# A two-layer cross-attention on one core: maxima transposed a slot later, even entries with their image tokens first, and one value product for two entries

## The chip, the cores and the metric

The kernel runs on one core of a Trainium2 chip. The time is device microseconds of one execution. The profile is of one execution of its own, whose time stands beside the others below.

## What is computed

Two cross-attention layers follow each other over 16 entries of 256 rows and 320 channels. Each entry has a context of 256 tokens of 512 channels. In layer 0 the first 77 tokens are text and the other 179 image tokens, with key and value weights of their own. In layer 1 252 are text and 4 image. The core of layer 0, from the reference (20 heads of 16 channels):

```python
q_h = _split_heads(q, B, HEADS, D)
k_h = _split_heads(k_text, B, HEADS, D)
probs = jax.nn.softmax(jnp.einsum('bhqd,bhkd->bhqk', q_h, k_h) * scale, axis=-1)
text_out = jnp.einsum('bhqk,bhkd->bhqd', probs, v_h)
scores = jnp.einsum('bhqd,bhkd->bhqk', q_h, ip_k_h) * scale
text_probs = jax.nn.softmax(jnp.einsum('bqc,bkc->bqk', q, k_text) * scale, axis=-1)
q_sem = jnp.einsum('bqk,bkc->bqc', text_probs, text)
sem = jnp.einsum('bqc,bnc->bqn', q_sem, ip) * scale
fused = scores + SEM_SCALE * sem[:, None, :, :]
ip_probs = jax.nn.softmax(fused, axis=-1) * spatial_mask[None, None, :, None]
ip_out = jnp.einsum('bhqk,bhkd->bhqd', ip_probs, ip_v_h)
out = (text_out + IP_SCALE * ip_out) @ Wout + bout + residual
```

So each head has two softmaxes over one row of scores, each with a maximum of its own, and the image scores get a term `sem` that is the same for all heads.

## The kernel before

Arithmetic is in f32 with most products split into a rounded high part and a remainder (`halves`, `split`, `evacuate`): a product of 128x320 over 512 channels is then a group of twelve matmuls (`prod`, L239).

**Slots.** A slot is one entry and one group of four heads. Layer 0 has slots 0 to 79 (five for an entry), layer 1 slots 80 to 159. `slot0(k)` writes one slot of layer 0 and does the work of three neighbours at once: the scores of slot k+2 in two halves (`score0`, L744) with the reduces that take their maxima over text and over image (DVE, L745 and L746), the transposed scores of slot k (`turned0`, L768), their `exp` (ACT, L771) and a product with the row factors (POOL, L774), and the attention of slot k−1 (`attend0`, L800, and `settle0`: DVE L811 to L817, POOL L818 and L820). The scores of `score0` have one tile of two banks, and the second half's scores use it after the first half's reduces.

**Maxima.** `maxima0(k)` transposes the reduced maxima on PE (L752), copies them on ACT (L754) and stores them with four transfers (L756, issued by ACT) into rows of the queries' stack Q. `turned0` of that slot then subtracts them in the same matmul. At the end of slot k the maxima of slot k+2 are handled, ahead of the background that is due by then. On ACT the second half's `exp` of slot k stays behind the four transfers of slot k+1 (`queued(exp, issues[k + 1])`).

**Background.** All other work of layer 0 is cut into steps with due times in slots (`task`, `fill`): of a pair of entries the keys (`keys0`), of an entry the queries (`queries0`, L609 and L612 on `hq`), token products `tokens0` of text with image tokens (tile M), the values (`values0_`: three groups of twelve matmuls for an entry, whose results ACT writes into the tile `vr`, L423), the semantic term (`semantic0`, L666, L685, L695), and the output projection (`close0`: L609 and L612 on `ho`, which ACT, then DVE split from the gathered attention at L282 to L284). A pair of entries takes ten slots, so the order of the background repeats every ten slots; "x2" below is slots 12, 22, 32 and so on. Context is loaded by pairs into tiles `cta` and `ctb` (`context`), split by ACT (L164) and POOL (L167). Keys go through a DRAM buffer (`kd`) into the stacks K (`ks`).

**What sets the order.** Up to slot 0 `begin()` is written out by hand, and every engine runs in the order written. In the slots, PE runs in the order written; the order of ACT, DVE, POOL and SP is chosen when the program is built, within what data and the edges of `anchor` and `queued` demand. An instruction marked `anchor` is one that later `queued` ones of its engine stay behind.

## Time and profile before

| | us |
|---|---|
| runs | 1503.99, 1501.08, 1503.84; median 1503.84 |
| profiled execution | 1502.55, span 1500.7, granted clock 0.990 |
| start-up (written out by hand) | 0 to about 66 of the span |
| slots 0 to 57 | about 66 to 515 |
| rest of layer 0 and the way into layer 1 | about 515 to 760 |

An engine in the profile runs its instructions in their order. A matmul waits for its operands at its place in the order of PE, so a wait that one shows is time in which PE does nothing. The name X is a tile of the matmul banks shared by the background work; S, T and P are the tiles of scores, of transposed scores, and of attention and probabilities. A tile's number in a name is left out by the profile, and kept in the rows of the order below.

### The profile page before, as it was taken

How to read it: one execution, taken by the hardware profiler on the slowest of the kernel's cores; microseconds unless marked ns; L12 is line 12 of the kernel's file. 1: busy time of each engine (PE TensorE's matmuls, PEld its weight loads, DVE VectorE, ACT ScalarE, POOL GpSimd, SP SyncE). 2: the span in 40 equal slices, each digit the busy share in tenths (PEclk: the TensorE clock that was granted, in tenths of full speed). 3: DMA queues.
4: the chain of work that ended last, by engine and by line, in shares of the span. 5: the costliest groups of instructions: out<-in, count | busy, mean ns of one | idle time of the engine just before them, and what ended most of it. 6: DMA issues, size and time to landing. Idle time of an engine off the chain costs nothing.

```text
span 1500.7 us, 36096 instructions
## 1 busy us (share of the span) xinstructions
PE 1422.2 (95%) x12740; PEld 1148.3 (77%) x12740; DVE 1179.7 (79%) x2593; ACT 889.5 (59%) x1975; POOL 1212.4 (81%) x1304
## 2 busy tenths in 40 slices
PE   8789999999999999789999999999999999999997
PEld 7678788888878877567777777777777777777765
DVE  5467777777778787878887788878877887788786
ACT  5356565656555655456665666566656665666563
POOL 4269797979787887898698779877987798779887
PEclk9799999999999999999999999999999999999999
DMA  7867777868676776774534434443444344433411
GB/s 234 202 200 211 199 221 196 226 190 223 185 207 193 219 217 167 199 214 145 165 99 130 124 116 118 131 128 112 121 131 128 110 122 127 130 109 99 121 30 44
DMA packets 230986, 234.32 MB, mean 156 GB/s; under 512 B 39127, under 2 KB 200678, under 8 KB 230790
## 3 DMA queue, kind: packets, MB, share of 16 engines
q1 hardware_dynamic: 228598, 230.71, 55.1%
q8 instruction: 102, 1.67, 0.5%
q10 hardware_dynamic: 2208, 1.30, 0.4%
q14 instruction: 78, 0.64, 0.1%
HBM read 118.04 MB, written 77.04 MB: 130 GB/s over the span
## 4 chain that ended last, share of the span: by engine, by line
PE 70%; DVE 13%; DMA 6%; POOL 5%; issue 3%; ACT 2%; SPq 1%; ACTq 0%; DVEq 0%; POOLq 0%
PE X L938 15%; PE X L239 14%; PE P L800 6%; PE X L609 5%; PE P L950 5%; PE P L960 4%; PE S L744 3%; PE T L890 3%; PE S L896 3%; DVE mn L746 3%; PE T L768 3%; PE X L612 2%; DVE nt L811 2%; PE X L578 2%; POOL P L774 1%
## 5 line engine op out<-in xcount | busy, mean ns | idle before, releaser
L774 POOL TENSOR_TENSOR P<-P,rs 128x512 f32<-128x512 f32 x320 | 413.7, 1314 | 89.8 <-ACT P L771 88.4
L929 POOL TENSOR_TENSOR wt<-P,ctb 128x512 f32<-128x512 f32 x320 | 410.7, 1307 | 74.0 <-ACT ctb L928 74.0
L938 PE MATMUL X<-ctb,gm 128*128 128x512 f32 x1120 | 305.4, 402 | 5.7 <-DVE wt L939 5.6
L771 ACT ACTIVATE P<-T 128x512 f32<-128x512 f32 x320 | 175.9, 595 | 151.1 <-PE T L768 120.6
L939 DVE TENSOR_TENSOR wt<-X,wt 128x512 f32<-128x512 f32 x320 | 216.5, 681 | 42.2 <-PE X L938 36.0
L938 PEld LDWEIGHTS X<-ctb,gm 128*128 128x128 f32 x1120 | 195.2, 188 | 39.0 <-DVE wt L939 8.6
L910 ACT ACTIVATE P<-T 128x512 f32<-128x512 f32 x320 | 173.2, 593 | 76.1 <-PE T L890 73.1
L928 ACT ACTIVATE ctb<-P 128x512 fp32r<-128x512 f32 x320 | 186.5, 627 | 38.9 <-PE X L938 33.5
L898 DVE TENSOR_REDUCE mn<-S 128x4 fp32r<-128x1008 f32 x160 | 191.5, 1197 | 0.0
L746 DVE TENSOR_REDUCE mn<-S 128x4 fp32r<-128x716 f32 x160 | 142.6, 891 | 0.0
L800 PE MATMUL P<-P,vr 128*32 128x256 f32 x1920 | 125.5, 392 | 7.2 <-DVE tmp L817 4.2
L744 PEld LDWEIGHTS S<-ks,qs 125*128 125x128 f32 x640 | 89.6, 194 | 39.9 <-issue 19.4
L744 PE MATMUL S<-ks,qs 125*128 125x256 f32 x640 | 114.4, 302 | 6.0 <-DMA ks<-M 3.7
L1027 POOL TENSOR_TENSOR r<-u,rs 128x40 f32<-128x40 f32 (+2 forms) x17 | 108.7, 6393 | 4.0 <-DVE u L1024 4.0
L745 DVE TENSOR_REDUCE mn<-S 128x4 fp32r<-128x308 f32 x160 | 74.9, 468 | 42.7 <-PE S L744 41.9
L768 PE MATMUL T<-qs,ks 127*128 127x256 f32 x640 | 105.5, 288 | 0.1
L800 PEld LDWEIGHTS P<-P,vr 128*32 128x32 f32 x1920 | 56.8, 112 | 48.2 <-issue 9.9
L768 PEld LDWEIGHTS T<-qs,ks 127*128 127x128 f32 x640 | 90.1, 194 | 0.9 <-issue 0.3
L950 PE MATMUL P<-P,v1t 128*32 128x256 f32 x1280 | 85.7, 385 | 0.0
L960 PE MATMUL P<-wt,zone 128*32 128x256 f32 x1280 | 84.6, 379 | 0.3 <-DVE wt L939 0.3
L811 DVE STREAM_TRANSPOSE nt<-P 128x512 f32<-128x512 f32 x80 | 57.0, 712 | 34.3 <-PE P L800 33.6
L239 PE MATMUL X<-wC,cta 128*128 128x324 f32 (+1 forms) x474 | 78.4, 312 | 0.0
(297 smaller groups left out, 2974.0 us busy)
## 6 DMA issues: line engine op xcount, KB each, us to landing
qd<-q SPq DMA_DIRECT2D x96, 256.0 KB
qs<-tph SPq DMA_DIRECT2D x64, 320.0 KB
rawc<-in_cT_dram SPq DMA_DIRECT2D x60, 256.0 KB
qs<-qd SPq DMA_DIRECT2D x80, 192.0 KB
ks<-kd SPq DMA_DIRECT2D x80, 192.0 KB
ks<-kd SPq DMA_DIRECT2D x160, 96.0 KB
qs<-qd SPq DMA_DIRECT2D x160, 96.0 KB
kd<-kst SPq DMA_DIRECT2D x57, 256.0 KB
```

What stands on the lines that cost most here:

```text
L239: last = mm(out, lhs(a, k), rhs(b, k), start=i == 0, stop=i == len(terms) - 1)
L744: mm(sp[:, h], Q[: XROW + T0, h, t * 128 : (t + 1) * 128], K[: XROW + T0, h], start=True, stop=True)
L746: anchor(nc.vector.tensor_reduce(mn[:, t, :, 1], sp[:, :, T0:], axis=AX.X, op=ALU.max))
L768: mm(st[p][:, j], K[:KS0, 2 * p + j, t * 128 : (t + 1) * 128], Q[:KS0, 2 * p + j], start=True, stop=True)
L771: exp = anchor(nc.scalar.activation(pt, st[p], AF.Exp, scale=SCALE))
L774: anchor(nc.gpsimd.tensor_mul(pt, pt, rs[:, t : t + 1].to_broadcast([128, 2, S])))
L800: mm(pv[32 * s : 32 * s + 32, o : o + S], v[:, vt, h : h + 32], P[k, s // 2][:, t, s % 2], start=vt < 2, stop=vt != 1,)
L898: anchor(nc.vector.tensor_reduce(maxes[k + 2][:, t], sp[:, :, :T1], axis=AX.X, op=ALU.max))
L928: nc.scalar.activation(R[k, u][:, t], P[k, u][:, t], AF.Copy, scale=0.5)
L929: anchor(nc.gpsimd.tensor_sub(W[k, u][:, t], P[k, u][:, t], f(R[k, u][:, t])))
L938: mm(yp, gm[:, gb], R[k, u][:, kt], start=i == 0, stop=i == len(blocks[n]) - 1)
L939: nc.vector.tensor_mul(W[k, u][:, n], yp, W[k, u][:, n])
```

## The change

Five parts, all of them in layer 0:

1. **Maxima.** For slots 1 to 57 (`SOON`) the maxima of slot k+1 are handled as the first thing of slot k, after the background of the slot before, in place of the maxima of slot k+2 ahead of the background of slot k. From slot 57 on they are handled as before.
2. **Image first.** Even entries have their image tokens ahead of their text in the key stack (a view 77 columns further on, `turned_ks`, of a stack that is 77 columns wider), in the reduces, in the product with M, and in the order of the three value tiles in `attend0`.
3. **One product for two mixed tiles.** An entry's 256 tokens make a tile that has the text, a mixed one and one of image tokens alone for the value products. With the even entry turned around, the mixed tiles of both entries are the same 128 columns of the context tile, and one product serves both: `values_mixed` is one group of twelve matmuls, evicted twice with different masks (`emask`, `tmask`). A pair of entries needs five groups and not six. `mark` writes the masks' columns for an entry, where `marks` did it once.
4. **Context and keys by piece.** Context tiles are padded, with text at one place and images at another, so a loaded context tile is split in two pieces, by ACT and POOL, with edges between them. Image keys are evicted per entry in two pieces on ACT and DVE (128x179), and POOL copies the text keys for an entry at a time. The token product has 180 columns in place of 192, the text keys' product 154 in place of 156.
5. **Start-up.** `fields()` stores the ends of the wider stacks with four more transfers; the constants of the padded tiles are set by more than 20 small memsets on POOL. `tokens0` sets no columns to zero in the slots any more.

The core of the diff:

```diff
     def slot0(k):
+        if 0 < k <= SOON:
+            yield lambda: maxima(k + 1)
         yield lambda: ahead(k + 2, 0)
         yield lambda: turned0(k, 0)
         yield 0.2
...
         yield 0.6
-        yield lambda: maxima(k + 2)
+        if k >= SOON:
+            yield lambda: maxima(k + 2)
         yield 1.0
...
-        for t, (w,), lo, sc in ((0, wv0, 0, tmask[:, 0:1]), (1, wvi0, 0, tmask[:, 1:2]), (2, wvi0, 128, 1.0)):
-            vp = bank()[:, :320]
-            prod(vp, lambda s, k: ct(s, k)[:, i, lo : lo + 128], lambda s, k: w(s, k), 4)
+    def value_rows(ct, at, w, *to):
+
+        vp = bank()[:, :320]
+        prod(vp, lambda s, k: side(ct[k], s, at, 128), lambda s, k: w(s, k), 4)
+        for V, t, sc in to:
             nc.scalar.activation(
...
+    def values_mixed(c):
+        to = [(vr[(b + 2) % 3], 1, masks(b)[1]) for b in (2 * c, 2 * c + 1)]
+        value_rows(ct0[c], CI + 128, wvi0[0], *to)
+        yield
...
+    def evacuate(hi, lo, out, m, pieces=None):
+
+        cut = [lambda t, b=b: t[:, b] for b in pieces] if pieces else [lambda t: t]
+        if m == 2:
+            hi, lo = hi[:64], lo[:64]
+            both = buf("both", list(hi.shape), bufs=2)
+        for of in cut:
+            nc.scalar.copy(of(hi), of(out[:64] if m == 2 else out))
+        if m == 2:
+            nc.scalar.copy(both, out[64:])
+            out = out[:64]
+        for of in cut:
+            nc.vector.tensor_sub(of(out if m == 2 else lo), of(out), f(of(hi)))
+        if m == 2:
+            nc.vector.tensor_add(lo, out, both)
...
+        if loaded == "pieces":
+            order = lambda inst: anchor(queued(inst))
...
+                hi, lo, src = ahead.pop(0)
+                if isinstance(hi, list):
+                    for piece in zip(hi, lo, by_side(src)):
+                        halves(*piece, eng, "pieces")
...
-        task(("v0", 2 * c), shifted(n, -7, -5.4, -5), lambda b=2 * c: values0_(b), *k)
-        task(("v0", 2 * c + 1), shifted(n, -4, -3.8, -3.4), lambda b=2 * c + 1: values0_(b), *k)
+        task(("v0", 2 * c), shifted(n, -7, -5.4), lambda b=2 * c: values0_(b), *k)
+        task(("vm", c), shifted(n, -4.2), lambda c=c: values_mixed(c), *k)
+        task(("v0", 2 * c + 1), shifted(n, -3.8, -3.4), lambda b=2 * c + 1: values0_(b), ("vm", c))
```

**PE at the end of slot 29.** L752 (after: L845) is the transposes of the maxima, L685 (L776) a transpose of the semantic term, L609 (L700) a query projection; each row ends with the shape of one result and the count. Before, and then of the change:

```order
L768 MATMUL T<-qs_96,ks_100 128x256 x4
L752 MATMUL X<-ident_r,mn_567 8x128 x2
L685 MATMUL X<-ident,sp_376 77x128
L685 MATMUL X<-ident,sp_377 77x128
L609 MATMUL X<-hq_230,wE_86 128x256 x8
```
```order
L861 MATMUL T<-qs_96,ks_100 128x256 x4
L776 MATMUL X<-ident,sp_413 77x128
L776 MATMUL X<-ident,sp_414 77x128
L700 MATMUL X<-hq_270,wE_86 128x256 x8
L845 MATMUL X<-ident_r,mn_615 8x128 x2
```

The transposes of the maxima have moved behind the ten matmuls of the background. They now stand directly ahead of the scores of the next slot.

**PE at the end of slot 34.** L239 (L251) with the weights `wD` is the value products. Before, and then of the change:

```order
L768 MATMUL T<-qs_97,ks_101 128x256 x4
L239 MATMUL X<-wD,cta_81 128x320 x3
L239 MATMUL X<-wD,cta_82 128x320 x3
L239 MATMUL X<-wD,ctb_83 128x320 x3
L239 MATMUL X<-wD,ctb_84 128x320 x3
L752 MATMUL X<-ident_r,mn_566 8x128 x2
L239 MATMUL X<-wD,cta_81 128x320 x3
L239 MATMUL X<-wD,cta_82 128x320 x3
L239 MATMUL X<-wD,ctb_83 128x320 x3
L239 MATMUL X<-wD,ctb_84 128x320 x3
```
```order
L861 MATMUL T<-qs_97,ks_101 128x256 x4
L251 MATMUL X<-wD,cta_81 128x320 x3
L251 MATMUL X<-wD,cta_82 128x320 x3
L251 MATMUL X<-wD,ctb_83 128x320 x3
L251 MATMUL X<-wD,ctb_84 128x320 x3
L845 MATMUL X<-ident_r,mn_614 8x128 x2
```

One of two value groups is gone from this place, and the transposes stand at the end.

**DVE from slot 31 into slot 32.** L811 (after: L907) is the transpose of an attention result, L745 and L746 (L838 and L839) the reduces, L814, L815 and L817 (L910, L911 and L913) the rest of `settle0`, L830 (L926) gathers attention for the output projection, L283 and L284 (L326 and L327) split its operand `ho`, L260 and L261 (L276 and L278) evict the third part of keys and queries. The last two rows of before are the reduces of slot 32's first scores:

```order
L745 TENSOR_REDUCE mn_567<-S 128x4
L746 TENSOR_REDUCE mn_567<-S 128x4
L814 RECIPROCAL P<-nt_136 128x16
L283 TENSOR_TENSOR ho_161<-hT_1308,ho_161 128x512
L284 SCALAR_TENSOR_TENSOR ho_161<-ho_161,tmask,hT_1308 128x256
L815 TENSOR_TENSOR P<-P,mk 128x8
L260 TENSOR_TENSOR X<-X,kst_160 64x2x179
L817 TENSOR_TENSOR tmp_807<-nt_136,P 128x256
L745 TENSOR_REDUCE mn_566<-S 128x4
L746 TENSOR_REDUCE mn_566<-S 128x4
```

In the change the reduces of slot 32's first scores are the seventh and eighth row (tile `mn_614`), and the first row is the last reduce of slot 31:

```order
L839 TENSOR_REDUCE mn_615<-S 128x4
L910 RECIPROCAL P<-nt_137 128x16
L911 TENSOR_TENSOR P<-P,mk 128x8
L913 TENSOR_TENSOR tmp_850<-nt_137,P 128x256
L926 STREAM_TRANSPOSE hT_1337<-hsn 128x256
L276 TENSOR_TENSOR X<-X,kst_194 64x179
L838 TENSOR_REDUCE mn_614<-S 128x4
L839 TENSOR_REDUCE mn_614<-S 128x4
L276 TENSOR_TENSOR X<-X,kst_194 64x179
L276 TENSOR_TENSOR X<-X,q_146 64x256
L326 TENSOR_TENSOR ho_195<-hT_1337,ho_195 128x512
L327 SCALAR_TENSOR_TENSOR ho_195<-ho_195,tmask,hT_1337 128x256
```

`ho` has moved from ahead of slot 32's first reduces to behind them and behind two subtractions. PE's projection that reads it stands in slot 32 behind the first transposed scores, as before.

**DVE from slot 37 into slot 38.** L846 (after: L942) adds bias and residual of the output projection; the eviction of the queries' third part, L260 and L261 (L276 and L278), is read by the semantic product L666 (L757) of slot 38. Before, and then of the change:

```order
L817 TENSOR_TENSOR tmp_807<-nt_136,P 128x256
L260 TENSOR_TENSOR X<-X,q_145 64x256
L846 SCALAR_TENSOR_TENSOR xc_116<-X,bo,xc_116 128x256
L261 TENSOR_TENSOR q_145<-X,both_281 64x256
L745 TENSOR_REDUCE mn_566<-S 128x4
L746 TENSOR_REDUCE mn_566<-S 128x4
L846 SCALAR_TENSOR_TENSOR xc_116<-X,bo,xc_116 64x256
```
```order
L913 TENSOR_TENSOR tmp_850<-nt_137,P 128x256
L942 SCALAR_TENSOR_TENSOR xc_117<-X,bo,xc_117 128x256
L838 TENSOR_REDUCE mn_614<-S 128x4
L839 TENSOR_REDUCE mn_614<-S 128x4
L276 TENSOR_TENSOR X<-X,q_146 64x256
L942 SCALAR_TENSOR_TENSOR xc_117<-X,bo,xc_117 64x256
L278 TENSOR_TENSOR q_146<-X,both_319 64x256
```

L261 stood ahead of the reduces of slot 38's first scores; as L278 it stands behind them, behind L276 and the third part of L942.

More of the change, by code (lines that the diff above doesn't have):

```diff
@@ L394, in keys_first @@
         out = lambda lo, hi: bank()[:, : 2 * (hi - lo)].rearrange("p (b t) -> p b t", b=2)
-        kp = [out(0, T0 + 1) for m in range(3)]
+        kp = [out(0, T0) for m in range(3)]
         for k in range(4):
@@ L399, in keys_first @@
                 for i, (a, c) in enumerate(terms):
-                    mm(kp[m], wk0(a, k, m), ct(c, k)[:, :, : T0 + 1], start=k + i == 0, stop=k == 3 and i == len(terms) - 1)
+                    mm(kp[m], wk0(a, k, m), texts_of(ct[k], c), start=k + i == 0, stop=k == 3 and i == len(terms) - 1)
             yield
@@ L803, in values0 @@
                 P[k, s // 2][:, t, s % 2],
[L804 to L805 removed]
+                start=bool(start),
+                stop=bool(stop),
             )
```

185 lines of the change are left out of this document (119 added, 66 removed).

## Prediction

> **What bounds the kernel now.** I read the page's head and its shares of the chain first, then the busy time by stage, then PE's waits in the stage that the change touches.
>
> ```profile
> PE 1422.2 (95%) x12740; PEld 1148.3 (77%) x12740; DVE 1179.7 (79%) x2593; ACT 889.5 (59%) x1975; POOL 1212.4 (81%) x1304
> ...
> PE 70%; DVE 13%; DMA 6%; POOL 5%; issue 3%; ACT 2%; SPq 1%; ACTq 0%; DVEq 0%; POOLq 0%
> ```
>
> PE is busy 95% of the span and carries 70% of the chain, DVE 13%. By stage (columns: stretch, length, then busy time of PE, PEld, DVE, ACT and POOL, the granted clock, the DMA share, GB/s):
>
> ```profile
> 0.00:66.00 66.00, 48.38 (x286) 45.11 (x287) 34.17 (x97) 32.38 (x83) 23.46 (x45) 0.90 0.83 233
> 66.00:515.00 449.00, 428.50 (x4023) 366.54 (x4023) 338.98 (x773) 259.02 (x599) 371.36 (x361) 1.00 0.73 203
> ```
>
> The second row holds slots 0 to 57 of the first layer, where the changed order lies. PE idles 20.5 us of 449 there, POOL is busy 83%, DVE 75%. The second layer's order is left as it is. What PE waits for in slots 0 to 57 (us in total, times, longest):
>
> ```profile
> PE X L752 <- DVE mn L746: 12.3, 22, 0.8
> ...
> PE S L744 <- DVE mn L746: 0.2, 1, 0.2
> ```
>
> Over half of the idle time is the transposes of the maxima waiting for the reduces of the scores ahead of them. So there are two ways to gain: fewer matmuls, and that wait. There is one large way to lose: another engine's result that PE now meets too early.
>
> **The maxima, moved.** One such wait, at the end of slot 29, PE first and DVE after it:
>
> ```profile
> 295.06 0.22 PE L752 MATMUL X<-ident_r,mn 128*8 128x128 f32 x1
> 296.12 0.23 PE L752 MATMUL X<-ident_r,mn 128*8 128x128 f32 x1 [0.84 <-DVE mn L746]
> 296.18 0.39 PE L685 MATMUL X<-ident,sp 128*77 128x128 f32 x2
> 296.33 1.18 PE L609 MATMUL X<-hq,wE 128*128 128x256 f32 x8
> 297.35 0.64 PE L744 MATMUL S<-ks,qs 125*128 125x256 f32 x4
> ```
> ```profile
> 295.17 0.90 DVE L746 TENSOR_REDUCE mn<-S 128x4 fp32r<-128x716 f32 x1
> ```
>
> The second transpose waits 0.84 us for a reduce that ends at 296.07. In the new order the ten matmuls of L685 and L609 stand ahead of both transposes: 297.35 − 296.18 = 1.17 us of cover. The reduce is then done, and the wait goes. The other slots of the ten-slot cycle get their background group in front in the same way. I take the whole row: **−12.3 us**. The bounds are 0 (the wait turns up elsewhere) and −12.3. The four transfers that follow (L756) leave later, and `exp` of the slot's second half is queued behind them on ACT; the TURN that needs them comes most of a slot later, and a slot lasts 7.8 us (from slot 32 to 38 in the rows below, 359.23 − 312.29 for six). That is why I cost this delay at nothing. If the cover were thinner than I think, each late landing would stop TURN.
>
> **Fewer matmuls.** The value groups in slot 34, and the token group behind them:
>
> ```profile
> 331.80 1.04 PE L239 MATMUL X<-wD,cta 128*128 128x320 f32 x6
> ...
> 333.57 0.29 PE L752 MATMUL X<-ident_r,mn 128*8 128x128 f32 x2
> 333.69 1.10 PE L239 MATMUL X<-wD,cta 128*128 128x320 f32 x6
> ...
> 335.50 0.64 PE L744 MATMUL S<-ks,qs 125*128 125x256 f32 x4
> ...
> 336.46 0.70 PE L239 MATMUL X<-cta 128*77 128x192 f32 x6
> ...
> 337.62 1.07 PE L800 MATMUL P<-P,vr 128*32 128x256 f32 x16
> ```
>
> A group of twelve 320-column matmuls takes 333.57 − 331.80 = 1.77 us, or 335.50 − 333.69 = 1.81. Eight groups go, one for each pair of entries; the first lies in the start-up stretch, where PE waits for transfers anyway. Seven times 1.81 rounded up for the issue between groups is **−12.9 us**. The evictions stay as many, since each entry still gets its own. The token group takes 337.62 − 336.46 = 1.16 us for 192 columns; at 180 it is 12/192 of that, 0.07 us, for 14 groups; **−0.9 us** with the text keys' 154 columns in place of 156.
>
> The gains sum to 12.3 + 12.9 + 0.9 = **26.1 us**.
>
> **What now waits for DVE: the output projection.** The order of DVE has changed most at slots 12, 22, 32, 42 and 52. Slot 32 in the trace of before:
>
> ```profile
> 312.29 0.63 PE L744 MATMUL S<-ks,qs 125*128 125x256 f32 x4
> ...
> 313.25 1.43 PE L609 MATMUL X<-ho,wF 128*128 128x256 f32 x8
> ...
> 315.10 1.27 PE L800 MATMUL P<-P,vr 128*32 128x256 f32 x18 [0.43 <-DVE tmp L817]
> ```
> ```profile
> 311.29 1.39 DVE L283 TENSOR_TENSOR ho<-hT,ho 128x512 fp32r<-128x512 f32 x1
> 312.60 1.52 DVE L284 SCALAR_TENSOR_TENSOR ho<-ho,tmask,hT 128x256 fp32r<-128x256 f32 x1
> ```
>
> DVE starts `ho` at 311.29, a microsecond before slot 32 begins, so the projection L609 runs almost unhindered. In the new order `ho` stands behind the reduces of slot 32's own scores and two subtractions of 64 rows. How soon the reduces end after their scores is seen where DVE idled before them, in slot 37:
>
> ```profile
> 352.00 0.64 PE L744 MATMUL S<-ks,qs 125*128 125x256 f32 x4
> ```
> ```profile
> 353.08 0.90 DVE L746 TENSOR_REDUCE mn<-S 128x4 fp32r<-128x716 f32 x1
> ```
>
> That is 353.98 − 352.00 = 1.98 us after the scores start. So in slot 32: 312.29 + 1.98 = 314.27. The two subtractions and `ho` cost:
>
> ```profile
> L260 DVE TENSOR_TENSOR X<-X,q 64x256 f32<-64x256 f32 x17 | 7.1, 420 | 7.3 <-ACT both L259 7.3
> ...
> L260 DVE TENSOR_TENSOR X<-X,kst 64x154 f32<-64x154 f32 x7 | 2.2, 318 | 5.5 <-ACT both L259 5.5
> ...
> L283 DVE TENSOR_TENSOR ho<-hT,ho 128x512 fp32r<-128x512 f32 x16 | 21.4, 1336 | 7.2 <-ACT ho L282 7.2
> ...
> L284 DVE SCALAR_TENSOR_TENSOR ho<-ho,tmask,hT 128x256 fp32r<-128x256 f32 x16 | 15.9, 995 | 0.0
> ```
>
> With about 0.08 us of each overlapping the next, these are 0.32 + 0.34 + 1.26 + 0.95 = 2.9 us, so `ho` is complete near 317.2 (317.7 with the 1.52 us that L284 took in this slot). The projection's last matmuls take another half microsecond, and the attention L800 starts at 317.7 to 318.2 in place of 315.10: **2.6 to 3.1 us, taken as 2.9, in five slots: +14.5 us.** The bounds are 0 a slot (if the scheduled order is not what holds PE) and 3.1.
>
> **A second, smaller wait of that kind** lies at slots 8, 18, 28, 38 and 48. Slot 38 before:
>
> ```profile
> 359.23 0.64 PE L744 MATMUL S<-ks,qs 125*128 125x256 f32 x4
> ...
> 360.77 0.79 PE L666 MATMUL X<-kb,q 128*128 128x156 f32 x6
> 361.50 1.50 PE L800 MATMUL P<-P,vr 128*32 128x256 f32 x24
> ```
> ```profile
> 360.04 0.41 DVE L261 TENSOR_TENSOR q<-X,both 64x256 fp32r<-64x256 f32 x1
> ```
>
> The sixth matmul of L666, near 361.37, reads what L261 has written by 360.45. In the new order L261 comes behind the reduces of slot 38's scores (359.23 + 1.98 = 361.21), a subtraction of 0.42, L846 of 0.46 and its own 0.41, less 0.08 each: it ends near 362.35. That is 1.0 us late, five times: **+5.2 us** (bounds 0 and 6). The even entries' `ho` also moves to the end of slot x6, where the second half's scores of slot x7 can wait for the reduces behind it, 0 to 0.4 us each: **+1 us**.
>
> **Start-up.** Four more transfers are issued on SP's queue within a stretch that runs without a gap and lies on the chain:
>
> ```profile
> 18.00 3.67 SPq L84 DMA_DIRECT2D ks<-mt  x4
> ```
>
> Four like them are 3.67 us. SP is in the chain in pieces between landings, so I take about half, **+2.0 us** (bounds 0 and 3.7). The additional small memsets and context pieces run on POOL and ACT, which are busy 23 and 32 of those 66 us.
>
> **The rest costs nothing where it is hidden.** Keys in two pieces instead of one give ACT and DVE a second short operation each, on engines with at least a quarter idle; what that does to their order is counted above. POOL gets more: the context subtraction in two pieces, two small copies an entry, twice the key copies, less one memset.
>
> ```profile
> POOL P L774 <- ACT P L771: 60.1, 60, 4.7
> ```
> ```profile
> L384 POOL CAST kb<-kst 128x308 fp32r<-128x308 f32 x14 | 6.2, 441 | 0.0
> ...
> L820 POOL COPY hsn<-hsn 128x128 f32<-128x128 f32 x16 | 4.8, 302 | 0.8
> ```
>
> From the last two rows a column costs (441 − 302)/(308 − 128) = 0.77 ns, so the fixed part of an operation is some 0.2 us. Four pieces, four copies and three key copies, less two memsets, are nine of these, 1.8 us in a cycle of ten slots. POOL has 17% of 78 us free, 13 us, and most of that is waiting for `exp` (60.1 of the 77.6 us that it idles in this stretch, first row). I count nothing; the bounds are 0 and the price under the rivals.
>
> **The sum.** Losses: 14.5 + 5.2 + 1.0 + 2.0 = 22.7 us. Net −26.1 + 22.7 = **−3.4 us** against the profiled execution's 1502.55 us (span 1500.7): 1499.2. The median of the runs is 1503.84, 1.3 above that execution; on it the forecast is **1500.5 us**.
>
> **A page against the trace.** Alone in the start-up, a DVE subtraction of 128x512 with two SBUF inputs takes 692 ns, while the same shape in L283 takes 1336 with POOL at work:
>
> ```profile
> L1263 DVE TENSOR_TENSOR cta<-rawc,cta 128x512 fp32r<-128x512 f32 x2 | 1.4, 692 | 3.4 <-ACT cta L1256 3.4
> ```
>
> The Trainium skill, page "SBUF — State Buffer", section "SBUF: two separate sides", says that DVE and GpSimd share one pair of ports as an exclusive lock, and that the loser waits until the whole instruction is done. The two rows agree with it. By that rule POOL, which runs out of work while PE stands still in slots 12 to 52, would leave the port to `ho`, which would then cost 0.65 us less: 5 × 0.65 = 3.2 us less loss, 1497.3. I do not take it, since POOL has `exp` of the same slot to multiply at that moment. The same skill, page "Perfetto Trace Analysis", section "Optimizing Scalar/DVE Operations", says that breaking up instructions may let work complete sooner where an engine isn't saturated but causes bubbles; that speaks for the pieces and against my costing their order as a loss.
>
> **The rivals.**
>
> *The gains arrive whole.* DVE and PE shift against each other, `ho` comes early enough, and only the start-up is lost: 1503.84 − 26.1 + 2.0 = **1479.7 us**. For it: DVE is only 75% busy in this stretch. Against it: an engine runs its list in order, and the list has `ho` behind reduces that can't start before slot 32's scores. Chance 0.15; half of the losses would give 1491.
>
> *POOL becomes the bound (the slower side).* In slots 25 to 29 it works almost without a gap, and its lead over PE is small:
>
> ```profile
> 285.75 5.21 POOL L774 TENSOR_TENSOR P<-P,rs 128x512 f32<-128x512 f32 x4
> ```
> ```profile
> 292.57 1.50 PE L800 MATMUL P<-P,vr 128*32 128x256 f32 x24
> ```
>
> Slot 28's products end at 290.96 and its attention starts at 292.57: 1.6 us ahead. In such a stretch PE would gain about 2.2 of a cycle's 26.1/7 = 3.7 us, and POOL be charged 1.8; from 1.6 us on, each further microsecond stops PE. That gives back 4.0 − 1.6 = 2.4 us a cycle, and in four cycles (the first starts with POOL ahead) 9.6 us: **1510.1 us**. Against it: PE's new stalls at x2 and x8 give POOL time. Chance 0.17.
>
> *The change doesn't remove the wait.* The score tile has one buffer, so the next scores need the same reduces that the maxima waited for; the wait moves to L744: +12.3, **1512.8 us**. Against it: those scores wait 0.2 us in all today, behind 1.2 to 1.8 us of other matmuls. Chance 0.08.
>
> *The maxima land late.* Transfers issued up to 1.8 us later hold TURN or ACT's queue, 0.1 us a slot: 57 × 0.1 = 5.7, **1506.2 us**. Chance 0.10.
>
> **How the numbers follow.** My forecast has 0.50. Its own terms reach from 1490 (the `ho` stall at half) to 1506 (a start-up at 3.7, later waits at their bounds). The range goes from 1485 to 1511: of the cases outside it, the whole gain and the wait that only moves, about 0.2 is left out. A difference of 0.2%, 3 us, is what a measurement can tell from none. Faster by more (below 1500.8): half of the forecast, 0.27, the first rival 0.15, and a few of the rest, 0.46. Within: 0.20 of the forecast and 0.07 of late maxima, 0.27. Slower (above 1506.8): 0.17 + 0.08 and the tail, 0.27.
>
> **What would show it.** In the trace of the changed kernel, the wait of the maxima's transposes for the reduces should be gone up to slot 57 and stay beyond it. The projection reading `ho` should wait for DVE some 2.9 us in slots 12, 22, 32, 42 and 52; the product with the text keys (L666 in before) about 1 us in slots x8. PE should have 96 matmuls fewer. The start should be 2 us longer up to the first attention. If `ho` does not hold PE, or POOL's idle time falls under 5% in slots x5 to x9, the prediction is wrong by that term.

## The result, and the profile after

| | before | changed |
|---|---|---|
| median (lowest to highest), us | 1502.88 (1501.08 to 1505.82) | 1514.45 (1508.53 to 1516.88) |
| profiled execution: time, span, granted clock | 1502.55, 1500.7, 0.990 | 1508.53, 1506.8, 0.982 |

The ratio is 1.0060, with an interval of 1.0045 to 1.0074: the change costs about 9 us by the ratio (the medians lie 11.6 us apart). The forecast was 1500.5, and the range ended at 1511. The profiled execution of the changed kernel is the fastest of its six, so a second trace of the same program, 1516.7 us long, stands beside it below ("the change again").

From the page of the changed kernel: the first row has the engines' busy time, the second their shares of the chain.

```profile
PE 1420.0 (94%) x12644; PEld 1144.5 (76%) x12644; DVE 1173.7 (78%) x2625; ACT 888.6 (59%) x2031; POOL 1223.0 (81%) x1391
...
PE 70%; DMA 11%; DVE 8%; POOL 3%; issue 3%; ACT 2%; SPq 2%; ACTq 1%; DVEq 0%; POOLq 0%
```

PE has 96 matmuls fewer, as forecast, yet is busy only 2.2 us less. The busy time by stage, in the columns of before, says why:

```profile
0.00:66.00 66.00, 48.23 (x270) 45.36 (x271) 34.12 (x107) 32.99 (x94) 24.40 (x73) 0.84 0.80 227
66.00:515.00 449.00, 423.88 (x3952) 362.06 (x3952) 334.57 (x791) 257.28 (x638) 378.08 (x411) 0.98 0.76 203
```

In slots 0 to 57 the idle time grew from 20.5 to 25.1 us, and the clock fell from 1.00 to 0.98: part of the work that is left runs slower. The waits of PE in that stage:

```profile
PE X L700 <- ACT ho L325: 6.3, 5, 1.3
PE X L251 <- DVE sp L760: 2.7, 1, 2.7
PE X L757 <- ACT mt L847: 2.5, 2, 1.3
PE X L700 <- DVE ho L326: 2.3, 5, 0.5
PE X L757 <- DVE q L278: 2.2, 3, 0.8
PE S L836 <- DMA qs<-mt: 1.9, 2, 1.1
...
PE T L861 <- DMA qs<-mt: 1.1, 3, 0.6
```

The wait of the maxima's transposes, 12.3 us in 22 waits of at most 0.8, is gone in this trace. In its place stand fewer and longer ones: the output projection (L700), the text keys' product (L757), one wait of 2.7 us (L251) that no step had, and 3.0 us for the transfers of the maxima, for which the kernel before does not wait here at all.

To see where the time went I cut each trace into windows of half a microsecond and added up three things: time in which PE did nothing, PE's busy time multiplied by (1 − granted clock), and the rest, which is the matmuls at full clock.

| profiled execution, us | span | PE idle | lost to half clock | matmuls at full clock |
|---|---|---|---|---|
| before | 1500.7 | 77.7 | 13.4 | 1409.7 |
| changed | 1506.8 | 86.2 | 24.0 | 1396.8 |
| the change again | 1516.7 | 91.6 | 27.1 | 1397.9 |
| forecast difference | | +10.4 | 0 | −13.8 |
| measured differences | | +8.5, +13.9 | **+10.6, +13.7** | −12.9, −11.8 |

Two columns came out near the forecast, the idle time of the second trace 3.5 us above it. The column of half clock was not in the sum at all.

By place: at the attention of slot 57 the changed kernel's first trace is 1.0 us behind before (0.9 of it from the start-up), where the forecast's terms, less the one product group that comes later, have it 1.6 us ahead; the second trace is 8.7 us behind. The rest, 5.1 and 7.3 us, comes later, and 4.3 and 2.7 us of that in layer 1, whose order the change leaves as it is. Why layer 1 took longer is not shown.

**One long wait, row by row.** In slot 9 of the changed kernel, PE first, then DVE, then POOL:

```profile
141.00 2.15 PE L251 MATMUL X<-cta,wB 128*128 128x360 f32 x6 [2.72 <-DVE sp L760]
```
```profile
136.88 3.92 DVE L327 SCALAR_TENSOR_TENSOR hq<-hq,tmask,xq 128x256 fp32r<-128x256 f32 x1
140.73 0.22 DVE L760 TENSOR_TENSOR sp<-sp,X 128x77 f32<-128x77 f32 x1
```
```profile
133.63 5.01 POOL L867 TENSOR_TENSOR P<-P,rs 128x512 f32<-128x512 f32 x4
138.60 1.25 POOL L326 TENSOR_TENSOR hq<-xq,hq 128x512 fp32r<-128x512 f32 x1
139.82 0.45 POOL L914 TENSOR_TENSOR hsn<-tmp 128x128 f32<-128x128 f32 x1
140.22 0.31 POOL L464 CAST kb<-kst 128x154 fp32r<-128x154 f32 x1
```

DVE's L327 is a short operation: on the same shape it takes 0.47 us in slot 32 below. Here it lasts 3.92 us and ends when POOL's gapless row of seven instructions ends (140.22 + 0.31 = 140.53). The small subtraction that PE needs stands behind it. What follows on PE (columns as in the stages above, clock third from the end):

```profile
140.00:141.00 1.00, 0.00 (x0) 0.00 (x0) 1.00 (x4) 0.00 (x0) 0.53 (x2) 1.00 0.93 146
141.00:142.00 1.00, 1.00 (x3) 1.00 (x4) 1.00 (x4) 0.94 (x3) 0.34 (x2) 0.53 1.00 197
142.00:143.00 1.00, 1.00 (x5) 1.00 (x5) 0.73 (x3) 0.60 (x2) 1.00 (x1) 0.50 0.71 203
143.00:144.00 1.00, 1.00 (x5) 1.00 (x4) 0.16 (x1) 0.24 (x2) 1.00 (x2) 0.50 0.01 2
145.00:146.00 1.00, 1.00 (x24) 0.49 (x16) 0.59 (x2) 0.71 (x3) 0.00 (x0) 1.00 0.00 0
```

PE works again from 141.0, but at half clock until about 144.5. The wait is 2.72 us; with the half clock, and a wait of 0.84 us for L278 ahead of it, slots 8 and 9 came out 5.3 us longer.

**The forecast stall, row by row.** Slot 32, where the projection was to wait 2.9 us. PE, then DVE:

```profile
316.19 0.64 PE L861 MATMUL T<-qs,ks 127*128 127x256 f32 x4
318.08 0.39 PE L700 MATMUL X<-ho,wF 128*128 128x256 f32 x1 [1.26 <-ACT ho L325]
318.92 1.08 PE L700 MATMUL X<-ho,wF 128*128 128x256 f32 x7 [0.45 <-DVE ho L326]
```
```profile
316.80 0.88 DVE L839 TENSOR_REDUCE mn<-S 128x4 fp32r<-128x716 f32 x1
317.61 0.33 DVE L276 TENSOR_TENSOR X<-X,kst 64x179 f32<-64x179 f32 x1
318.20 0.67 DVE L326 TENSOR_TENSOR ho<-hT,ho 128x512 fp32r<-128x512 f32 x1
318.80 0.47 DVE L327 SCALAR_TENSOR_TENSOR ho<-ho,tmask,hT 128x256 fp32r<-128x256 f32 x1
```

The order was as forecast: `ho` behind the reduces of the same slot. The wait is 1.26 + 0.45 us, not 2.9. The first matmul waits for ACT's part of `ho` (0.83 us, behind the copy of the maxima), which the forecast had left out, and DVE then does its two parts in 0.67 and 0.47 us where I took 1.26 and 0.95. POOL was waiting for `exp` from 317.3 to 318.6 and then began its own product. The Trainium skill's rule that I set aside (page "SBUF — State Buffer", section "SBUF: two separate sides") was the right one in this slot: 0.67 us for an operation that began while POOL stood idle, against 1336 ns on average before. POOL's own product, which started at 318.60 while DVE held on, took 1.82 us in place of 1.28.

### The profile page after: what moved, and what is told of

It reads as the page before. It is cut to its first block, busy times and chain, and to the rows that moved or that the text cites. A ratio compares the mean times of both kernels' runs of the same rounds, so it can differ in the third digit from the quotient of the medians.

```text
span 1506.8 us, 36169 instructions
## 1 busy us (share of the span) xinstructions
PE 1420.0 (94%) x12644; PEld 1144.5 (76%) x12644; DVE 1173.7 (78%) x2625; ACT 888.6 (59%) x2031; POOL 1223.0 (81%) x1391
## 4 chain that ended last, share of the span: by engine, by line
PE 70%; DMA 11%; DVE 8%; POOL 3%; issue 3%; ACT 2%; SPq 2%; ACTq 1%; DVEq 0%; POOLq 0%
PE X L1034 15%; PE X L251 12%; PE P L896 6%; PE X L700 6%; PE P L1046 5%; PE P L1056 4%; PE S L836 4%; PE S L992 3%; PE T L986 3%; PE T L861 3%; DMA qs<-mt 3%; PE X L261 2%; PE X L669 2%; DMA ks<-kd 2%; PE X L703 1%
## 5 line engine op out<-in xcount | busy, mean ns | idle before, releaser
L839 DVE TENSOR_REDUCE mn<-S 128x4 fp32r<-128x716 f32 x160 | 142.4, 890 | 0.0
L836 PE MATMUL S<-ks,qs 125*128 125x256 f32 x640 | 119.4, 310 | 9.0 <-DMA ks<-kd 2.4
L836 PEld LDWEIGHTS S<-ks,qs 125*128 125x128 f32 x640 | 89.9, 197 | 45.2 <-issue 25.1
L838 DVE TENSOR_REDUCE mn<-S 128x4 fp32r<-128x308 f32 x160 | 75.0, 469 | 34.8 <-PE S L836 34.3
L907 DVE STREAM_TRANSPOSE nt<-P 128x512 f32<-128x512 f32 x80 | 57.1, 713 | 54.2 <-PE P L896 53.7
L700 PE MATMUL X<-ho,wF 128*128 128x256 f32 x512 | 75.0, 287 | 10.7 <-ACT ho L325 7.2
```

The source lines that it names most:

```text
L836: mm(sp[:, h], Q[: XROW + T0, h, t * 128 : (t + 1) * 128], K[: XROW + T0, h], start=True, stop=True)
```

## The experiments

Ratios are to the kernel before, with their interval. Line numbers in rows are those of the kernel named.

**The change again**, without an edit.

> The changed kernel once more, for a second trace. Theory W (PE's new waits, and behind some of them stretches at half the granted clock, about 4 us each at some 2 us of loss): 1508 to 1517 us, the same waits at slots x2 and x8 as in the first trace, but the half-clock stretches in the slots behind other ones of these waits than at 141, 243 and 473 us. Rival L (something of the program itself, at a fixed place, lowers the clock): the same three places.

1514.99 us, 1.0075 [1.0048, 1.0101]. Single executions reach from 1507.94 to 1520.06. In its trace DVE's L327 was stopped in slot 9 and in slots 19, 29 and 49 too (3.78 us in slot 19, where POOL's row is 213.64 to 220.6). In the first trace a gap of 0.39 us in POOL's row (215.43 to 215.82) had moved that row against DVE's: L327 started at 216.98, as one of POOL's instructions was ending (217.11), and took 0.48 us, while POOL's next product took 1.56 us in place of 1.28. So DVE got in there without a gap. In the second trace the transposes of the maxima also wait for the reduces again, three times (2.5 us in slots 0 to 57), and the scores behind them 2.2 us. One program thus has times 12 us apart; its two traces differ in which of these meetings DVE loses and in where half clock falls.

**Which part?** `b_max` is the kernel before with part 1 alone:

```diff
     def slot0(k):
+        if 0 < k <= SOON:
+            yield lambda: maxima(k + 1)
...
-        yield lambda: maxima(k + 2)
+        if k >= SOON:
+            yield lambda: maxima(k + 2)
```

> The kernel before with the moved maxima alone (part 1). In its order on DVE ho stays ahead of slot 32's reduces, as in before. Theory W: the 12.3 us of waits in slots 1 to 57 go and nothing takes their place, 1489 to 1494. Rival M (the move itself puts waits elsewhere, on the next scores or on the landing of the maxima): 1500 to 1506.

1497.69 us, 0.9969 [0.9948, 0.9991]: a gain of about 5 us, where the wait that it removes is 12.3. Its waits in slots 0 to 57:

```profile
PE X L610 <- ACT mt L755: 4.0, 5, 0.8
PE X L240 <- DVE sp L670: 2.6, 2, 2.5
PE X L753 <- DVE mn L747: 1.6, 1, 1.6
```

The maxima's waits went, but single ones of 1.6 us (slot 3, half clock behind it, +3.25 us), 2.5 us (slot 9, which the expectations below count as slot 8; DVE's `hq` stopped for 3.64 us) and 2.4 us (slots 57 and 58, where the two orders meet, +4.2 us) came.

`a_nomax` is the changed kernel without part 1, the same edit backwards.

> The changed kernel with the maxima handled as before (parts 2 to 5 alone). Its order on DVE also has ho ahead of slot 32's reduces, so it is the two parts together that move it. Theory W: start-up +3, product groups -13, the maxima's waits unchanged, no wait for ho: 1492 to 1499. Rival P (pieces, marks and key copies on POOL and ACT cost more than the groups save): 1503 to 1512.

1521.27 us, 1.0113 [1.0086, 1.0139], slower than the whole change. My theory that the waits for `ho` hold the gain back falls here: DVE has `ho` early again, but now beside POOL. Slot 36, DVE, POOL and PE:

```profile
354.41 1.50 DVE L326 TENSOR_TENSOR ho<-hT,ho 128x512 fp32r<-128x512 f32 x1
355.83 1.51 DVE L327 SCALAR_TENSOR_TENSOR ho<-ho,tmask,hT 128x256 fp32r<-128x256 f32 x1
```
```profile
352.82 5.64 POOL L867 TENSOR_TENSOR P<-P,rs 128x512 f32<-128x512 f32 x4 [1.63 <-ACT P L864]
```
```profile
358.60 0.23 PE L845 MATMUL X<-ident_r,mn 128*8 128x128 f32 x1 [1.58 <-DVE mn L839]
```

The two parts of `ho` take 3.0 us in place of 1.1, the reduces come behind them, and PE waits 1.58 us there.

**`ho` early by order.** `a_ho` is the changed kernel with edges that put ACT's and DVE's parts of `ho` ahead of the maxima's copy and of the reduces at slots x2, and POOL's copy of the gathered attention ahead of the next slot's products.

> The changed kernel with three edges for odd entries (and POOL's for all): POOL copies the gathered attention before it starts the next slot's products, ACT and DVE split ho before the maxima's copy and the reduces of slots 12, 22 and so on. Theory W: five waits of 1.7 us and the half clock behind some of them go, 1499 to 1506. Rival P: DVE or POOL is late anyway and the wait moves by a few instructions, 1510 to 1516.

1514.96 us, 1.0077 [1.0051, 1.0103]: no gain. The wait at x2 halved, and others came:

```profile
PE X L251 <- DVE sp L764: 6.9, 5, 2.7
PE X L707 <- ACT mt L855: 6.4, 4, 1.8
```

`a_whole` evicts the image keys of the changed kernel whole (without `range(2)` in the call of `evacuate`), which also brings `ho` ahead of the reduces; `a_whole77` has the early maxima up to slot 77 besides, and `b_soon77` is `b_max` up to slot 77.

> The changed kernel with the image keys of both entries evicted in one operation again (all else of the change stays). In its order ho is ahead of the reduces in slots 12 to 52, as in before. Theory W: five waits of 1.7 us and the half clock behind them go, 1502 to 1508. Rival L: ho meets POOL's work there and takes 3 us instead of 1.1, the maxima wait for it, and the time is as before this edit, 1512 to 1517.

> The same with the moved maxima up to slot 77. What the step from 57 to 77 brings here beside what it brings to the kernel before tells whether the two add up: 0 to 8 us less than with 57.

> The kernel before with the moved maxima up to slot 77 instead of 57. Theory W: the 4.2 us lost in slots 57 and 58 of the kernel with the move up to 57, where both ways of handling the maxima meet, come later or not at all, and 7 us of waits beyond slot 57 go in part: 1489 to 1495. Rival: the loading of layer 1's weights holds these slots anyway, 1496 to 1500.

`a_whole`: 1526.05, 1.0144 [1.0113, 1.0174]; `a_whole77`: 1521.82, 1.0125 [1.0095, 1.0156]; `b_soon77`: 1502.90, 0.9995 [0.9978, 1.0012], with single executions from 1493.9 to 1508.1. In `a_whole` the wait for `ho` is gone, and DVE's last part of `hq` still takes up to 3.95 us. An earlier place in DVE's order does not help as long as POOL works there.

**Does POOL stop DVE?** `a_hqpool` gives `hq`'s last part, the operation stopped in slot 9, to POOL in both layers; `a_hq0` in layer 0 alone; `b_hq0` is `b_max` with the edit of `a_hq0`.

```diff
-        order(nc.vector.scalar_tensor_tensor(hl[:, 2], f(hl[:, 2]), neg, src[:, 2], op0=ALU.mult, op1=ALU.add))
+        if tag == "hq" and clock[0] < 70:
+            order(nc.gpsimd.tensor_sub(hl[64:, 2], src[64:, 2], f(hl[64:, 2])))
+        else:
+            order(nc.vector.scalar_tensor_tensor(hl[:, 2], f(hl[:, 2]), neg, src[:, 2], op0=ALU.mult, op1=ALU.add))
```

> The changed kernel with the last part of the queries' operand hq made by POOL (a subtraction on 64 partitions) and not by DVE. Theory L (a DVE operation with two operands in SBUF stands still while POOL works without a gap, and PE behind it): the wait of 2.7 us in slot 9 and the half clock behind it go, 1507 to 1511 us. Rival P (POOL is what lacks time, 17 more operations there cost more): 1514 to 1520.

> The changed kernel with hq's last part on POOL in layer 0 alone. Theory L: no stop of DVE in slot 9 nor in the slots x9, so slots 0 to 57 are 5 to 10 us shorter than in the changed kernel's two traces, layer 1 is as before: 1506 to 1512. Rival P (other operations of DVE stop instead, or POOL's added work holds slots x5 to x9): 1513 to 1519.

> The kernel before with the moved maxima and with hq's last part on POOL in layer 0. Theory L: the 2.5 us that slot 8 lost with the moved maxima do not come, 1492 to 1496. Rival P: 1497 to 1502.

`a_hqpool`: 1525.82, 1.0157 [1.0133, 1.0181]. The stop of slot 9 is gone, and by slot 56 the kernel is 4.4 us ahead of before; then slots 57 to 79 lose 13 us and layer 1 another 14, about 1 us an entry, with the additional operation on POOL. `a_hq0`: 1512.67, 1.0064 [1.0042, 1.0086], the same as the change, although no split of `hq` or `ho` on DVE lasts over 1.52 us in layer 0 of its trace. So the long stops of `hq` alone do not make the loss: the waits for `ho` (6.8 us) and for the maxima's transfers (5.2 us) stay, and half clock with them. `b_hq0`: 1542.20, 1.0261 [1.0241, 1.0281], which I had not expected, and it shows best how POOL holds DVE up. Slot 18, POOL, DVE and PE:

```profile
206.24 1.28 POOL L169 TENSOR_TENSOR cta<-rawc,cta 128x512 fp32r<-128x512 f32 x1
207.49 0.46 POOL L826 TENSOR_TENSOR hsn<-tmp 128x128 f32<-128x128 f32 x1
207.90 1.27 POOL L169 TENSOR_TENSOR cta<-rawc,cta 128x512 fp32r<-128x512 f32 x1
209.13 2.48 POOL L779 TENSOR_TENSOR P<-P,rs 128x512 f32<-128x512 f32 x2
```
```profile
205.91 6.25 DVE L285 TENSOR_TENSOR ho<-hT,ho 128x512 fp32r<-128x512 f32 x1 [1.36 <-ACT ho L284]
```
```profile
213.81 0.58 PE L749 MATMUL S<-ks,qs 125*128 125x256 f32 x1 [4.43 <-DVE mn L751]
```

POOL works from 203.7 to 211.6 without a gap. A DVE subtraction that takes 0.67 us beside an idle POOL starts at 205.91 and ends at 212.16, half a microsecond after POOL's last. Five times in slots 0 to 57, PE waits over 4 us for the reduces behind it, and half clock comes each time.

The last pair takes POOL's gapless work away: its product with the row factors in layer 0 covers half of the columns, in the changed kernel (`a_light`) and in the kernel before (`b_light`).

```diff
-            anchor(nc.gpsimd.tensor_mul(pt, pt, rs[:, t : t + 1].to_broadcast([128, 2, S])))
+            anchor(nc.gpsimd.tensor_mul(pt[:, :, :128], pt[:, :, :128], rs[:, t : t + 1, :128].to_broadcast([128, 2, 128])))
```

> The changed kernel with POOL's product of the row factors in layer 0 on half of the columns; the factors of the other columns are left out. POOL's gapless stretches of some 5 us in slots 0 to 57 should go, and with them DVE's stops. Theory L (what takes the gain is DVE stopped for as long as POOL works without a gap): no DVE operation of the split of hq or ho over 2.2 us, the idle time of PE between slots 0 and 57 falls from 17 to 21 us to under 12, and the kernel comes out 10 to 20 us faster than the kernel before with the same lighter POOL. Rival (the order of DVE and ACT alone takes it): the waits at slots x2, x7 and x8 stay, idle time stays at 16 us or more, and it is level with the lighter kernel before, within 5 us.

> The kernel before with POOL's product of the row factors in layer 0 on half of the columns; the factors of the other columns are left out. It is the partner of the lighter changed kernel. Theory L: the maxima's waits for the reduces stay in part, since they follow from the order; 1490 to 1500 us. Rival: the same as the kernel before within 3 us.

`a_light`: 1482.37 us, 0.9867 [0.9852, 0.9882]; `b_light`: 1486.94, 0.9883 [0.9863, 0.9904], lower than expected, so the kernel before also pays for POOL. From the first attention to that of slot 57, `a_light`, then `b_light`:

```profile
69.50:496.00 426.50, 414.87 (x3966) 357.42 (x3969) 329.03 (x796) 258.57 (x641) 257.63 (x417) 1.00 0.80 215
```
```profile
66.50:506.50 440.00, 425.57 (x4030) 366.31 (x4029) 333.49 (x776) 256.92 (x599) 250.97 (x364) 1.00 0.75 208
```

The same slots take 13.5 us less with the change: 10.7 of PE's busy time and 2.8 of idle time, with the clock at 1.00 in both. No split on DVE lasts over 1.61 us in layer 0, and `ho` has returned ahead of the reduces of slot x2. That much is theory L. But the distance at the end is only 4.6 us in the medians (7.8 in the traces), and the two intervals overlap, so the end does not tell the pair apart: the start-up gives 2.9 back, and slots 58 to 79, where both spend some 21 us at half clock, another 4.4. The size expected at the end, 10 to 20 us, was not reached, and that number is the rival's; its waits are not there. The light kernels change POOL's time and, through it, the order that is chosen, so the pair shows the two together; order alone, with POOL whole, failed in `a_nomax`, `a_ho` and `a_whole`. Nor did the 12.3 us of the maxima arrive whole: `b_light` has 9.2 us of them, and `a_light` is only 2.8 us less idle, since small waits for ACT and transfers take their place.

**What half clock costs.** `b_late` is the kernel before with DVE's first part of `ho` moved behind the reduces of slot x2, as the change does, and nothing else of it. Besides the edge shown, the first step of that entry's output projection is due at 7.1 slots in place of 6.

```diff
-        order(eng.tensor_sub(hl[:, 3:5], src[:, 0:2], f(hl[:, 0:2])))
+        late = queued if tag == "ho" and clock[0] < 60 else order
+        late(eng.tensor_sub(hl[:, 3:5], src[:, 0:2], f(hl[:, 0:2])))
```

> The kernel before with one edge: in slots 12, 22, 32, 42 and 52 DVE takes its first part of ho behind the reduces of that slot's first scores, as the changed kernel does. Theory W with the clock: five waits of about 1.4 us, and the half clock behind one to three of them at 2.3 us: 1509 to 1516 us. Rival V (a wait costs its own length): 1508 to 1510 and no half clock between 75 and 515 us.

1512.99 us, 1.0071 [1.0046, 1.0095]. Five waits, four of 1.70 us and one of 3.2, 10.0 us in all; half clock follows three of them. Other waits shrank, so against the trace of before PE idles only 3.1 us more in the whole trace, while 9.2 us more are lost to half clock: 5.1 of them in slots 10 to 57, most of the others in slots 57 to 79. One, PE and then the clock:

```profile
317.26 1.21 PE L610 MATMUL X<-ho,wF 128*128 128x256 f32 x7 [1.70 <-DVE ho L284]
318.40 2.79 PE L801 MATMUL P<-P,vr 128*32 128x256 f32 x24
```
```profile
318.00:319.00 1.00, 1.00 (x12) 0.54 (x14) 0.90 (x2) 0.00 (x0) 1.00 (x2) 0.55 0.93 262
319.00:320.00 1.00, 1.00 (x16) 0.40 (x11) 0.00 (x0) 0.00 (x0) 0.58 (x1) 0.50 0.90 216
320.00:321.00 1.00, 1.00 (x12) 0.19 (x4) 0.00 (x0) 0.00 (x0) 0.00 (x0) 0.50 0.36 83
```

The attention L801 takes 2.79 us; in the trace of before 24 such matmuls take 1.50.

`b_dose` and `b_dose2` put waits of graded length into layer 1 of the kernel before, which has no half clock otherwise up to its last microsecond. `b_dose` cuts each wait up by small matmuls; `b_dose2` has a single wait, for 1, 3, 5, 7 or 9 small copies on ACT:

```diff
+    def chain(n):
+        x = bank()[:, :2]
+        mm(x, ident, ident[:, :2], start=True, stop=True)
+        z = buf("mx", [128, 2], bufs=2)
+        for i in range(n):
+            nc.scalar.copy(z, x)
+        mm(bank()[:, :2], ident, z, start=True, stop=True)
...
     def slot1(k):
+        if k >= 90 and k % 3 == 0 and k < 150:
+            yield lambda: chain(2 * (k // 3 % 5) + 1)
```

> The kernel before with 12 chains put into layer 1 (slots 90, 95 to 145), where its trace shows no half clock at all: PE multiplies two columns, ACT copies them, PE needs the copy, one to four links in turn. Their result is not used. They make waits of PE of about 0.8 us a link. Theory C (the half clock follows from how much PE idles within a few microseconds, at a phase that is not the program's): behind one link (0.8 us) never, behind two (1.6) at some, behind three and four (2.4 and more) at nearly all, each half-clock stretch 3 to 4 us long and worth about 2 us: 24 us of waits and 10 to 16 of clock, 1537 to 1543 us. Rival (the clock falls for another reason, as at transfers or at the weights' loading): no half clock in layer 1, 1524 to 1529.

> The kernel before with 20 single waits in layer 1 (slots 90, 93 to 147): PE multiplies two columns, ACT copies them 1, 3, 5, 7 or 9 times over, PE needs the last copy; nothing else of PE lies in between. The result is not used. Waits of about 0.6, 1.0, 1.4, 1.8 and 2.2 us, four of each. Theory C: no half clock behind waits under 1.2 us, behind some of those of 1.4 to 1.8 and nearly all of 2.2, at different ones in the four places of one length. Rival: none at all, as behind the chains with links of 0.25 to 0.4 us, and the clock falls in layer 0 for another reason.

`b_dose`: 1524.24, 1.0135 [1.0107, 1.0164]; its chains came out at 0.41 to 1.16 us of idle time each, in pieces of 0.25 to 0.41, and half clock followed 1 of 12. I had expected 0.8 us a link, so this run says little about long waits that are cut up. `b_dose2`: 1580.13, 1.0510 [1.0489, 1.0531]. Its twenty waits:

| single wait, us | times | half clock after it | us at half clock each time |
|---|---|---|---|
| 0.40 | 4 | 0 | |
| 1.36 to 1.37 | 4 | 2 | 3.4 |
| 2.03 to 2.08 | 8 | 6 | 3.4, once 6.8 |
| 3.21 to 3.66 | 4 | 4 | 3.4 or 6.8 |

One of 2.03 us that ends at 1195.1, in windows of 2 us:

```profile
1193.00:1195.00 2.00, 0.08 (x1) 0.00 (x0) 1.34 (x3) 1.85 (x8) 2.00 (x2) 1.00 0.44 98
1195.00:1197.00 2.00, 1.88 (x18) 1.22 (x22) 1.02 (x2) 0.81 (x3) 1.59 (x3) 0.75 0.40 97
1197.00:1199.00 2.00, 2.00 (x24) 0.96 (x20) 0.27 (x1) 0.34 (x1) 0.00 (x0) 0.50 0.33 90
1199.00:1201.00 2.00, 2.00 (x21) 1.19 (x14) 1.18 (x6) 0.87 (x2) 0.55 (x3) 0.90 0.70 211
```

The clock falls about 0.9 us after PE is back at work, and is whole again by 1199.4. Such a stretch costs 1.7 us, a double one 3.4: nearly the wait over again.

Where the wait falls goes far to decide it. In all 20 traces the starts and ends of half clock lie on a grid of 3.413 us, to within 3 ns, which begins at another moment in each execution. Two of the four waits of 1.36 us lie within one step of the grid, and half clock follows both; the other two are split between two steps, and it follows neither. One of each kind, in windows that are steps of the grid (the second window is the half clock; the wait of the last two windows is split between them):

```profile
823.93:827.34 3.41, 2.04 (x29) 1.52 (x31) 2.67 (x7) 2.21 (x8) 3.33 (x5) 1.00 0.74 216
827.34:830.75 3.41, 3.41 (x35) 1.85 (x24) 1.45 (x6) 0.96 (x3) 0.92 (x2) 0.50 0.45 115
```
```profile
991.19:994.60 3.41, 2.94 (x21) 2.62 (x19) 3.28 (x9) 2.48 (x7) 3.41 (x4) 1.00 0.21 24
994.60:998.01 3.41, 2.52 (x39) 1.77 (x42) 2.39 (x6) 1.86 (x6) 3.31 (x5) 1.00 0.78 239
```

The same holds in `b_late`: its longest wait, 3.2 us, is split (PE busy 1.88 and 1.73 us of two steps) and no half clock follows, while three waits of 1.70 us that lie within one step are followed by it.

**What did not help.** `b_warm` adds 104 small matmuls to the start-up's waits of the kernel before; `a_actq` lets ACT issue the change's four additional start-up transfers; `b_e10` is `b_max` with early maxima from slot 11 on.

> The kernel before with 104 matmuls of the identity with itself, whose result nobody reads, put into three waits of PE in the start-up (ahead of the first scores, of the first maxima and of slot 0). Theory C (the half clock follows PE's waits): the stretch of half clock from 56 to 71 us goes or gets much shorter, and slots 0 and 1 take 3 to 4 us less: 1497 to 1501. Rival D (the start-up waits for transfers and DVE, the clock costs nothing there): 1502 to 1506.

> The changed kernel with the four additional transfers of the start-up issued by ACT instead of SP. If SP's queue makes the start-up longer: attention of slot 0 starts 2 to 3 us earlier than in the changed kernel, 1510 to 1513 us. Rival (the pieces of context and keys, or a phase of the clock): no change, 1513 to 1517.

> The kernel before with the moved maxima, from slot 11 on instead of slot 1. Theory W: what slots 3 and 8 lost in the trace of the moved maxima alone (3.3 and 2.5 us with the half clock behind) is not lost, 1489 to 1494 us. Rival L2 (such losses come from an order on DVE and POOL that meets POOL's long stretches somewhere in any case): they turn up in slots 11 to 20, 1496 to 1500.

`b_warm`: 1505.97, 1.0027 [1.0010, 1.0044], with the half clock of the start still there. `a_actq`: 1517.26, 1.0094 [1.0064, 1.0125], and the start no shorter. `b_e10`: 1498.49, 0.9974 [0.9956, 0.9993]: the losses of slots 3 and 9 (8 in the expectation) are gone, and one of the same kind stands at slot 19 (a wait of 2.5 us and half clock, +3.8 us).

## Why the prediction was wrong

- **Matmuls (−12.9 and −0.9): right.** Measured −12.9 and −11.8 at full clock.
- **Maxima (−12.3): the mechanism was right, the size was not.** The wait is gone up to slot 57 in the first trace, all but 2.5 us of it in the second; moved alone (`b_max`), the maxima gave about 5 us. The traces of the light pair show that small waits fill most of the room it leaves. Where the two orders meet, at slots 57 and 58, the transposes wait once more (2.4 us in `b_max`, 2.2 in `a_light`), which the sum had not. And the later transfers, put down at nothing, cost 3.0 us of waits in the first trace and 2.3 in the second: the rival of maxima that land late, at about half its size.
- **`ho` (+14.5): right place, too large.** 1.26 + 0.45 us of waiting, a net 1.1 to 1.6 us in each of five slots, 7 in all. I took DVE's durations from rows where POOL was at work, and left out ACT.
- **x8 (+5.2): right in place and nearly in size**: five waits, 4.7 us in all, though two of them are for ACT's copy of the maxima. The prediction's own figures give five times 0.9 to 1.0, so 4.5 to 4.9. (Another small slip there: half of the losses on top of the whole gain makes 1489, not 1491.)
- **Start-up (+2.0): the size is open.** The first attention comes 0.9 us later (69.2 for 68.3), made of 3.1 us more lost to half clock, 0.2 more idle and 2.3 less of matmuls. `a_actq` did not confirm that the four transfers' issue is the price.
- **POOL ("I count nothing"): failed.** I asked whether PE would wait for POOL's products; it hardly did. POOL's gapless work stops DVE's splits instead, and DVE stops PE. Rows of slot 9, `a_nomax` and `b_hq0` show it; `a_hq0`, without such stops of `hq`, is no faster than the change, and the light pair shows POOL's time and the order together. The sign set for this, an idle share of POOL under 5% in slots x5 to x9, did not appear: it fell from 10 to 14% to 5 to 9%.
- **The step that failed in the sum** is that each wait was put down at its own length. Net idle time was forecast at +10.4 and measured at +8.5 and +13.9. The change swaps 22 waits of at most 0.8 us, behind which the clock never fell, for waits of 1.2 to 2.7, behind which it often does. Half clock cost +10.6 and +13.7 us in all, 5.9 and 7.5 of it in slots 0 to 57, where from slot 3 on every fall comes after one of these waits (three in the first trace, four in the second). `b_late` has five such waits and no other part of the change, and is slower by 0.7%. The rest lies outside these slots: in both traces in the start-up (+3.1 us) and the last 20 us (+1.7), in the second also in slots 57 to 79 (+1.6). No run here tests what brings it there.

Why the same wait lowers the clock in one place and not in another can be read from the traces. Cut on the grid of 3.413 us, the 20 traces have 8433 steps at full clock. Half clock follows 127 of the 135 in which PE was busy less than half of the step, 49 of the 289 between 50 and 70%, and 4 of the 8009 above that. So what a wait costs depends on its place on the grid, and that differs between executions of one program. What stays open is what else decides between 50 and 70%, and which of the meetings of DVE and POOL end badly, since that too differs between executions.

The fastest version of the whole computation here is `b_max`, 1497.69 us, faster than both kernels; `b_e10`, at 1498.49, is not told apart from it.

## What to carry to other kernels

Many short waits of PE that lie apart can be cheaper than a few long ones of the same sum: here half clock came where PE was idle for about half of 3.4 us or more. So add up what PE idles within any 3.4 us, and price a new wait above about 1.2 us with a chance of 1.7 us of half clock behind it. Where a step leaves DVE an operation with two SBUF inputs, look at POOL's row at that moment, and not only at POOL's share of busy time. A change that moves an order chosen by the program trades one such meeting for another, so judge it by more than one trace.

## What the runs showed of the hardware

- Half clock after single waits (PE idle for 0.5 us or more, with no other such stretch within 7 us, from 80 to 1490 us of all 20 traces): under 1.2 us 3 of 321, 1.2 to 1.3 us 14 of 44, 1.3 to 1.6 us 5 of 39, 1.6 to 2.0 us 7 of 18, 2.0 us and more 25 of 31. Of those from 1.6 to 2.0 us, 7 of the 10 that lie within one step of the grid of 3.413 us were followed by it, and none of the 8 that are split between two. The Trainium skill, page "TensorE: Matmul & The Clock Gate", section "Part 1: The HAM clock gate", says that the clock halves after an idle window of about 3.4 us that runs freely. The stretches of 3.41 us, or 6.83, and the grid on which they lie agree with such a window; waits of 1.36 us that bring it about do not agree with a window that must be idle throughout.
- DVE stopped for longer than one POOL instruction: 3.92 and 6.25 us, through five and six of them, until POOL had a gap; but 0.48 us in slot 19 of the first trace, where DVE came between two of POOL's instructions and the second took 1.56 us in place of 1.28. The page "SBUF — State Buffer" of the Trainium skill has the loser wait for one whole instruction; the rows of the two long stops show a whole row of them.
